# Layer 0's preparation: statistics from whole rows, weights by chunks, a compact bias table, scales spread from rows

## The chip, the core and the metric

The kernel runs on one core of one Trainium2 chip. The metric is the device time of one execution in microseconds. A core has five engines with queues of their own: PE (matrix products, with its weight loads shown as PEld), DVE (vector), ACT (scalar), POOL (general) and SP (which here only issues DMA transfers). ACT and POOL issue transfers too. An engine works through its queue in order, and waits at the head of the queue hold up everything behind.

## The reference

The input x is float32 of shape (4, 8, 512, 512). Four layers follow, each of the form x = x + layer(group_norm(x)). Layer 0, the only one that the change touches, is a spiking attention over T = 4 time steps, B = 8 images, N = 512 rows and D = 512 columns with H = 8 heads of 64. Its core is:

```python
def lif(x):            # over the time steps, state v
    v = v + (xt - v) / 2
    spike = v >= 1
    v = v * (1 - spike)

q = heads(lif(bn(x @ Wq.T, ...)))       # k and v likewise
scores = einsum('tbhnd,tbhmd->tbhnm', q, k) * D ** -0.5
scores = scores + bias_table[rel]       # rel = m - n + N - 1, per head
out = einsum('tbhnm,tbhmd->tbhnd', scores, v)
out = lif(out) * gate_scale + gate_shift
out = lif(bn(out @ Wp.T, ...))
```

Group normalisation takes the mean and the variance of two images (a group of G = 4 groups) at one time step. `bn` is batch normalisation with given statistics: g * (x - m) / sqrt(v + eps) + b. Layers 1 to 3 are convolutions of 13 x 13, 3 x 3 (quantised) and 3 x 3.

## The kernel before

`network` calls `layer0`, then the class `Layer1`, then `layers23`. Layer 0 works through 32 steps of one image b and one time step t, with t inside b. A step has four parts: the projections v, k and q (each 4 row or column chunks of 4 float32 products, in `project_in`), the attention (`attend`), and the output projection with the residual (`project_out`). In program order the attention of step n is followed by the projections of step n + 1, with the output projections of step n between them. A framework orders the instructions: it simulates the engines and on each engine issues, at any moment, the earliest instruction of the program that is ready, an instruction whose buffer isn't free being passed over. The order that comes out is fixed in the program. `tc.issue_after(op)` adds one rule: instructions of the block that run on the engine of `op` stand behind `op` there.

What the first steps need, and where it is in the code:

- **Batch norms** (`batch_norms`, L314 on): the 18 columns of parameters give `a_half` (half the scale, 4 projections x 4 chunks of 128 features) and `c_half` (half the offset), with the features on the partitions.
- **Scales along the free dimension** (`along_free`, L329 on): v, k and p need scale and offset along the columns, the same on all partitions. For each of the 4 chunks DVE multiplies the identity by a column of `a_half` or `c_half` (`diag`, L336, two buffers), and PE multiplies a matrix of ones by it (L337) into one PSUM bank, `ps_free`. `prepare_in` (L346 on) multiplies the weights of v or k by the scale (DVE, L349) and stores twice the offset as `c_twice` (ACT, L350). The weights of q are used as they are: its scale is on the partitions.
- **Weights** (`load_weights`, L304 on): the transposed matrix goes to `wT[n]`, 128 partitions x 4 chunks x 512. Partition q * 32 + a of chunk c holds row q * 128 + c * 32 + a. Each of four transfers fills one quarter q of the partitions, for all chunks.
- **The image of a step** (`load_quarters`, L417 on): it is loaded in four quarters, in pieces of 512 bytes, into a layout in which DVE transposes blocks of 32 x 32 (`transposed`, L477 on). One buffer, "xq". `transpose` first normalises it (L618).
- **Statistics** (`statistics`, L605 on): `bn_stats` on each of four pieces of both images of the group (`count`, L431), then two small PE products over the partitions, and a power on POOL (`group_stats`, L177 to L197). Image 0's pieces are taken from its quarters, the other image's from whole row chunks `xs` of 128 rows x 512, which share the 6 buffers of tag "x" with the residual's chunks `xr`.
- **Bias planes** (`prepare_bias`, L354 on): the bias of head h is a Toeplitz matrix. For `toep` it is split into three bf16 parts whose sum is the float32 value, for each of 8 heads as 128 partitions x 896 elements, in which partition p holds the table shifted by p. The kernel before loads each head's shifted rows in float32 (`hankel`), and then splits: ACT rounds (L365), DVE subtracts (L366), ACT rounds the rest (L367), POOL subtracts (L368), ACT rounds again (L369). `hankel` and `rest` have room for two heads each. They are in the space of tags "h_o" and "h_p", which become states of neurons afterwards.
- **Output weights** (`prepare_out`, L376 on): 32 small PE products give the `shift` that gate_shift brings (L382), DVE makes the offset `c` of it (L390 to L392), which is spread and stored as `c_twice["p"]` (L394). Then the scale is spread to `scale_p` (L398), and four chunks `wp_k` are scaled (DVE, L401) and split into two parts (ACT L405, DVE L406, ACT L407). `scale_p` and `wp_k` share the three buffers of tag "v" with the potentials of all neurons (`v_v`, `v_k`, `v_q`, `v_o`). The loaded `wp32` is in the buffer that later holds the attention's spikes `so`.
- **Bands for layer 1** (`bands1`, L709 on): their scratch takes the "h_p" space after the bias planes, and one PE product (L741) waits for loads into it.

The two matrix products of `attend` for a pair of heads j go into `ps_a` (one bank, L527) and `ps_b` (two banks, 24 products, L535); ACT copies `ps_a` into `v_o` at t = 0 (L545), and DVE adds `ps_b` (L550).

The order around the change is this one, in `layer0`:

```python
load(0)
load_weights("v", nc.sync)
statistics(0, 0, 0, as_rows(xs[0]))
statistics(0, 0, 1, load_x(1, 0, "xs"))
batch_norms()
for k in range(NC):
    transpose(0, k)
with tc.issue_after(prepare_in("v")):
    load_weights("k", nc.scalar)
    load_weights("q", nc.scalar)
```

After it come the projections of step 0. Their first product is followed by `prepare_in("k")` and the loads and statistics of the second time step; after the last follow `prepare_bias`, `prepare_out` and `bands1`, all held behind `prepare_in("k")`, the first product group and the first potential on their engines.

Of the kernel before, what the change touches and what calls it, by code (L numbers as in the profile page):

```python
# [34 lines left out]
F32 = mybir.dt.float32  # L35
# [8 lines left out]
P = 128  # L44
# [3 lines left out]
SQ = 32  # L48
# [218 lines left out]
def layer0(  # L267
# [36 lines left out]
    def load_weights(n, engine):  # L304
        rows = i[f"wT_{n}"].rearrange("(q c a) e -> q a c e", c=NC, a=SQ)
        for q in range(P // SQ):
            engine.dma_start(wT[n][q * SQ : (q + 1) * SQ], rows[q])
# [3 lines left out]
    ones = wpool.tile([P, P], F32, name="ones")  # L311
    nc.vector.memset(ones, 1.0)

    def batch_norms():  # L314

        neg_half = wpool.tile([P, 4, NC], F32, name="nh0")
        nc.vector.memset(neg_half, -0.5)
        nc.vector.tensor_scalar_add(a_half, bn[:, :, 3, :], EPS)
        nc.gpsimd.tensor_tensor(a_half, a_half, neg_half, op=ALU.pow)
        nc.vector.tensor_mul(a_half, a_half, bn[:, :, 0, :])  # L320
        nc.vector.tensor_scalar_mul(a_half, a_half, 0.5)
        c = c_half[:, :3, :]
        nc.vector.scalar_tensor_tensor(
            c, bn[:, :3, 2, :], -1.0, a_half[:, :3, :], op0=ALU.mult, op1=ALU.mult
        )
        nc.vector.scalar_tensor_tensor(
            c, bn[:, :3, 1, :], 0.5, c, op0=ALU.mult, op1=ALU.add
        )

    def along_free(cols):  # L330


        ps = ps_mm.tile([P, D], F32, tag="mm", name="ps_free")
        for c in range(NC):
            diag = work.tile([P, P], F32, tag="diag", name="diag", bufs=2)
            nc.vector.tensor_scalar_mul(diag, ident, cols[:, c : c + 1])  # L336
            nc.tensor.matmul(  # L337
                ps[:, c * P : (c + 1) * P], lhsT=ones, rhs=diag, start=True, stop=True
            )
        return ps  # L340

    def phases(x):
        return x.rearrange("p (v g) -> p g v", g=PH)

    def prepare_in(n):
        j = "qkvp".index(n)  # L346
        scale = along_free(a_half[:, j, :])
        for k in range(NC):
            nc.vector.tensor_mul(wT[n][:, k, :], wT[n][:, k, :], scale)  # L349
        return nc.scalar.mul(c_twice[n], along_free(c_half[:, j, :]), 2.0).ins  # L350

    def prepare_bias():


        n_u = toep[0].shape[2]
        table = i["table"]
        hankel = state.tile([P, 2, n_u], F32, tag="h_o", name="hankel")
        rest = state.tile([P, 2, n_u], F32, tag="h_p", name="rest")
        for h in range(H):
            src, r = hankel[:, h % 2, :], rest[:, h % 2, :]  # L360
            nc.scalar.dma_start(
                src, bass.AP(table.tensor, h * (2 * N - 1), [[1, P], [1, n_u]])
            )
            dst = [w[:, h, :] for w in toep]
            nc.scalar.copy(dst[0], src[:, ::-1])  # L365
            nc.vector.tensor_sub(r, src[:, ::-1], dst[0])  # L366
            nc.scalar.copy(dst[1], r)  # L367
            nc.gpsimd.tensor_sub(r, r, dst[1])  # L368
            nc.scalar.copy(dst[2], r)  # L369
# [6 lines left out]
    def prepare_out(wp32):  # L376
# [3 lines left out]
        for e in range(NC):  # L380
# [11 lines left out]
        nc.vector.scalar_tensor_tensor(c, bn[:, 3, 1, :], 0.5, c, op0=ALU.mult, op1=ALU.add)  # L392

        nc.scalar.mul(  # L394
            c_twice["p"].rearrange("p (g v) -> p g v", g=PH), phases(along_free(c)), 2.0
        )
        scale = work.tile([P, D], F32, tag="v", name="scale_p", bufs=3)
        nc.scalar.copy(scale, along_free(a_half[:, 3, :]))  # L398
# [243 lines left out]

    load(0)
    load_weights("v", nc.sync)
    statistics(0, 0, 0, as_rows(xs[0]))
    statistics(0, 0, 1, load_x(1, 0, "xs"))
    batch_norms()
# [7 lines left out]
    for n in range(-1, last + 1):  # L655
# [39 lines left out]
        if n < 0:  # L695
            with ExitStack() as behind:
                for op in first:
                    behind.enter_context(tc.issue_after(op))
                prepare_bias()
# [598 lines left out]
```

## Time and profile before

Three executions took 2936.95, 2939.79 and 2939.95 us. One more was profiled; the profile's times are from its first to its last instruction.

| what | us |
|---|---|
| median of three executions | 2939.79 |
| the profiled execution, its own time | 2938.79 |
| span of its profile | 2937.0 |
| PE busy in the span | 2833.3 (96%) |
| DVE busy | 2214.3 (75%) |
| POOL busy | 1035.3 (35%) |
| ACT busy | 551.2 (19%) |
| last output projection of layer 0 starts | 2049.3 |

Busy times are shares of the whole span. Stages differ in what limits them, so a stage is read by itself: how much of it each engine is busy, what the granted PE clock is, and what ended an engine's idle time. In the lists of instructions, a line names the engine, the line of the kernel, the operation, what it writes and reads, the count, and in brackets the idle time just before and what ended it. A letter q after an engine's name is its queue, where transfers are issued.

### The profile page before, as it was taken

Reading aid. Unit: us, or ns where it says so; the run is one execution under the profiler, and the core shown is the slowest. Engines: PE = TensorE matmul, PEld = TensorE weight load, DVE = VectorE, ACT = ScalarE, POOL = GpSimd, SP = SyncE. Lnnn points to the kernel's source line nnn. Section 1 sums busy time; section 2 is a strip of 40 time slices with the busy share of each in tenths; the row PEclk is TensorE's granted clock in tenths of the full one; section 3 lists DMA queues with packets and bytes.
Section 4 is the critical chain, followed back from the end, with each engine's and each line's share of the span. In section 5 each row is a group of like instructions: output and inputs, shape, how many; then the busy total and the mean of one; then the engine's idle time right before and its main releaser. Section 6 shows DMA issues by size and latency. Waiting matters only on the chain. (4 is left out here: it accounts for less than half of the span.)

```text
span 2937.0 us, 36614 instructions
## 1 busy us (share of the span) xinstructions
PE 2833.3 (96%) x12865; PEld 1303.7 (44%) x12865; DVE 2214.3 (75%) x3915; ACT 551.2 (19%) x859; POOL 1035.3 (35%) x1928
## 2 busy tenths in 40 slices
PE   6899999999999999999999999999999999589999
PEld 3454555554555545455455555455333333223334
DVE  7897788789779778878877886886655566887870
ACT  1300010011010001001001000110211112766664
POOL 3343234333234323323422433332211112676650
PEclk9899999999999999999999999999999999889999
DMA  7323322222222222222221122113877779698865
GB/s 180 97 81 81 76 58 66 66 73 77 69 61 70 71 75 73 58 66 66 76 68 46 49 54 55 51 42 95 226 194 216 201 208 247 142 204 209 222 171 147
DMA packets 323943, 322.10 MB, mean 110 GB/s; under 512 B 21639, under 2 KB 237391, under 8 KB 323647
## 3 DMA queue, kind: packets, MB, share of 16 engines
q1 hardware_dynamic: 261504, 236.70, 32.9%
q0 software_dynamic: 20192, 56.83, 6.2%
q10 hardware_dynamic: 42063, 26.23, 3.2%
q8 instruction: 101, 1.65, 0.2%
q14 instruction: 83, 0.68, 0.1%
HBM read 210.57 MB, written 103.60 MB: 107 GB/s over the span
## 5 line engine op out<-in xcount | busy, mean ns | idle before, releaser
L499 PE MATMUL ps_in<-w_v,xn 128*128 128x512 f32 x1024 | 459.7, 599 | 3.0 <-DVE xn L480 3.0
L499 PE MATMUL ps_in<-w_kq,xn 128*128 128x512 f32 x1024 | 450.2, 592 | 0.0
L815 PE MATMUL ps_conv<-x,bt 112*64 112x512 f32 x2048 | 445.1, 592 | 0.8 <-DVE v_p L467 0.8
L499 PE MATMUL ps_in<-xn,w_kq 128*128 128x512 f32 x1024 | 444.6, 592 | 0.0
L535 PE MATMUL ps_b<-toep,vtok 128*64 128x512 bf16 x3072 | 368.4, 383 | 1.0 <-DVE v_o L550 1.0
L475 POOL TENSOR_TENSOR h_v<-h_v,c_v 128x512 f32<-128x512 f32 x96 | 121.9, 1270 | 685.1 <-DVE h_v L474 659.4
L450 ACT ACTIVATE h_q<-v_q,c_half 128x512 f32<-128x512 f32 x96 | 69.2, 721 | 1473.0 <-DVE v_q L446 865.1
L584 POOL COPY x1s<-x1s 128x2 f32<-128x2 f32 (+1 forms) x1024 | 227.8, 278 | 272.8 <-DVE x1s L573 272.8
L562 PE MATMUL ps_out<-wp,so 128*128 128x512 f32 x1024 | 308.8, 444 | 0.0
L499 PEld LDWEIGHTS ps_in<-xn,w_kq 128*128 128x128 f32 x1024 | 194.3, 190 | 233.0 <-issue 222.0
L499 PEld LDWEIGHTS ps_in<-w_kq,xn 128*128 128x128 f32 x1024 | 194.2, 190 | 219.9 <-issue 205.0
L499 PEld LDWEIGHTS ps_in<-w_v,xn 128*128 128x128 f32 x1024 | 191.0, 191 | 218.6 <-issue 210.3
L815 PEld LDWEIGHTS ps_conv<-x,bt 112*64 112x64 f32 x2048 | 145.5, 135 | 289.7 <-issue 287.8
L1200 PE MATMUL ps_conv<-x,band_t 64*64 64x512 f32 x2040 | 252.5, 612 | 3.1 <-DVE band_t L1169 3.1
L1065 POOL COPY u<-x 128x512 f32<-128x512 f32 (+1 forms) x172 | 209.3, 1252 | 99.6 <-issue 51.8
L535 PEld LDWEIGHTS <-vtok 128*64 128x64 bf16 x3072 | 175.6, 111 | 154.7 <-issue 5.6
L562 PEld LDWEIGHTS ps_out<-wp,so 128*128 128x128 f32 x1024 | 192.6, 188 | 94.3 <-issue 58.3
L573 DVE SCALAR_TENSOR_TENSOR x1s<-v_p,xr 128x256 f32<-128x256 f32 x256 | 188.6, 776 | 13.9 <-DMA x<-x1s 3.1
L833 POOL DMA_DIRECT2D x<-xo x128 | 71.4, 565 | 313.7 <-ACT xo L822 299.4
L475 POOL TENSOR_TENSOR h_k<-h_k,c_k 128x512 f32<-128x512 f32 x96 | 123.2, 1283 | 135.1 <-DVE h_k L474 135.1
L822 ACT ACTIVATE xo<-ps_conv,off 128x512 f32<-128x512 f32 x128 | 87.9, 687 | 430.9 <-PE ps_conv L815 315.1
L1105 DVE SCALAR_TENSOR_TENSOR x<-ps_conv,inv,u 128x512 f32<-128x512 f32 (+1 forms) x172 | 121.7, 745 | 57.8 <-PE ps_conv L1098 30.6
(190 smaller groups left out, 3279.7 us busy)
## 6 DMA issues: line engine op xcount, KB each, us to landing
x<-x SPq DMA_DIRECT2D x64, 917.0 KB
x<-x SPq DMA_DIRECT2D x168, 256.0 KB
x<-x1s POOLq DMA_DIRECT2D x128, 262.0 KB, 2.6
xq<-in_x SPq DMA_DIRECT2D x128, 256.0 KB
xr<-in_x SPq DMA_DIRECT2D x128, 256.0 KB
out<-o SPq DMA_DIRECT2D x164, 192.0 KB
xs<-in_x SPq DMA_DIRECT2D x112, 256.0 KB
x<-xo ACTq DMA_DIRECT2D x128, 128.0 KB
```

The source lines that it names most:

```text
L475: nc.gpsimd.tensor_add(h, h, c_twice[n])
L499: mm = nc.tensor.matmul(ps, lhsT=lhsT, rhs=rhs, start=k == 0, stop=k == NC - 1)
L535: nc.tensor.matmul(pb[two * DH : (two + 1) * DH, :], lhsT=v[:, c, h * DH : (h + 1) * DH], rhs=toep[z][:, h, u : u + N], start=c == 0 and z ...
L562: nc.tensor.matmul(ps, lhsT=so[:, k, c * P : (c + 1) * P], rhs=wpT[z][:, k, :], start=k == 0 and z == 0, stop=k == NC - 1 and z == 1,)
L573: nc.vector.scalar_tensor_tensor(own, v.rearrange("p (g v) -> p g v", g=PH)[:, two, :], 1.0, by_phase[:, two, :], op0=ALU.is_ge, op1=ALU.add,)
L584: nc.gpsimd.tensor_copy(x1[:, f, u : u + n], x1[:, fm, um - n + 1 : um + 1][:, ::-1])
L815: mm = nc.tensor.matmul(ps[q * M1 : (q + 1) * M1, :], lhsT=bt[:, z, :], rhs=xt[:, w0 : w0 + N_PS1, z : z + NV], start=z == 0, stop=z == SH ...
L822: nc.scalar.activation(xo[:, a, :], ps, AF.Identity, bias=off[:, t : t + 1])
L833: engine.dma_start(bass.AP(dst.tensor, dst.offset + (q * n_half * W1_OUT * B + b) * D + f * NV, [[B * D, W1_OUT], [W1_OUT * B * D, n_half] ...
L1065: nc.gpsimd.tensor_copy(u[:n_p, j, :].rearrange("p (v g) -> p v g", g=PH), x[:, j, :].rearrange("p (g v) -> p v g", g=PH),)
L1105: done["DVE"] = nc.vector.scalar_tensor_tensor(own, ps[:n_p, :], w["inv"][:n_p], u[:n_p, j, :], op0=ALU.mult, op1=ALU.add, accum_out=sums[ ...
L1200: mm = nc.tensor.matmul(ps[j][b * HALF : (b + 1) * HALF, :], lhsT=band[half, b, dx, :], rhs=x3[half, s0 + j, dx : dx + D], start=dx == 0, ...
```

## The change

It touches five things, all in `layer0`:

- The statistics of the first time step are taken from whole row chunks of both images, so image 0 is loaded a second time as eight row chunks with the other image. These loads come before the quarters and the v weights in program order. `batch_norms` and the two transposes to rows come first of all, and the vector instructions of the block stand behind the last one of `batch_norms`.
- `load_weights` fills one chunk of all 128 partitions in each of its four transfers, for v, k and q.
- `along_free` takes rows: `as_rows_of` transposes the columns once on PE and copies them to SBUF on ACT, and PE then multiplies one column of the identity, repeated 128 times, by these rows.
- The bias table is split into its three parts in compact form, 24 partitions x 341 elements, on DVE (`split_bias`), and the parts are stored in DRAM. `prepare_bias` loads shifted rows of each part in bf16 for two heads at a time, and ACT copies them, reversed, to `toep`.
- In `prepare_out` the scale is spread before the offset.

```diff
     def load_weights(n, engine):
-        rows = i[f"wT_{n}"].rearrange("(q c a) e -> q a c e", c=NC, a=SQ)
-        for q in range(P // SQ):
-            engine.dma_start(wT[n][q * SQ : (q + 1) * SQ], rows[q])
+        rows = i[f"wT_{n}"].rearrange("(q c a) e -> c q a e", c=NC, a=SQ)
+        for c in range(NC):
+            engine.dma_start(wT[n][:, c, :], rows[c])
...
+    def as_rows_of(cols):
+        n = cols.shape[1]
+        ps = ps_mm.tile([n, P], F32, tag="mm", name="ps_rows")
+        nc.tensor.transpose(ps, cols, ident)
+        rows = wpool.tile([4 * NC, P], F32, tag="rows", name="rows", bufs=2)
+        nc.scalar.copy(rows[:n], ps)
+        return rows[:n]
+
+    def along_free(rows, j):
+        n = rows.shape[0]
         ps = ps_mm.tile([P, D], F32, tag="mm", name="ps_free")
         for c in range(NC):
-            diag = work.tile([P, P], F32, tag="diag", name="diag", bufs=2)
-            nc.vector.tensor_scalar_mul(diag, ident, cols[:, c : c + 1])
+            at = NC * j + c
             nc.tensor.matmul(
-                ps[:, c * P : (c + 1) * P], lhsT=ones, rhs=diag, start=True, stop=True
+                ps[:, c * P : (c + 1) * P], lhsT=ident[:n, at : at + 1].to_broadcast([n, P]),
+                rhs=rows, start=True, stop=True,
             )
...
-    def prepare_bias():
-        for h in range(H):
-            src, r = hankel[:, h % 2, :], rest[:, h % 2, :]
-            nc.scalar.dma_start(
-                src, bass.AP(table.tensor, h * (2 * N - 1), [[1, P], [1, n_u]])
-            )
-            dst = [w[:, h, :] for w in toep]
-            nc.scalar.copy(dst[0], src[:, ::-1])
-            nc.vector.tensor_sub(r, src[:, ::-1], dst[0])
-            nc.scalar.copy(dst[1], r)
-            nc.gpsimd.tensor_sub(r, r, dst[1])
-            nc.scalar.copy(dst[2], r)
+    def split_bias():
+        n_e = n_h // 3
+        parts = tc.dram_tile([3, H * n_h], BF16, name="bias_parts")
+        src = state.tile([3 * H, n_e], F32, tag="h_o", name="bias_table")
+        nc.scalar.dma_start(src, bass.AP(i["table"].tensor, 0, [[n_e, 3 * H], [1, n_e]]))
+        part = state.tile([3 * H, 3, n_e], BF16, tag="h_p", name="bias_part")
+        for z in range(3):
+            nc.vector.tensor_copy(part[:, z, :], src)
+            if z < 2:
+                nc.vector.tensor_sub(src, src, part[:, z, :])
+        nc.scalar.dma_start(
+            bass.AP(parts.tensor, parts.offset, [[n_e, 3 * H], [H * n_h, 3], [1, n_e]]), part
+        )
+        return parts
+
+    def prepare_bias(parts):
+        for h in range(0, H, 2):
+            for z in range(3):
+                hankel = state.tile(
+                    [P, 2, n_u], BF16, tag="h_o" if (h + z) % 2 else "h_p", name="hankel"
+                )
+                nc.scalar.dma_start(
+                    hankel,
+                    bass.AP(
+                        parts.tensor, parts.offset + (z * H + h) * n_h, [[1, P], [n_h, 2], [1, n_u]]
+                    ),
+                )
+                nc.scalar.copy(toep[z][:, h : h + 2, :], hankel[:, :, ::-1])
...
+        scale = work.tile([P, D], F32, tag="v", name="scale_p", bufs=3)
+        nc.scalar.copy(scale, along_free(a_rows, 3))
         nc.scalar.mul(
-            c_twice["p"].rearrange("p (g v) -> p g v", g=PH), phases(along_free(c)), 2.0
-        )
-        scale = work.tile([P, D], F32, tag="v", name="scale_p", bufs=3)
-        nc.scalar.copy(scale, along_free(a_half[:, 3, :]))
+            c_twice["p"].rearrange("p (g v) -> p g v", g=PH), phases(along_free(as_rows_of(c), 0)), 2.0
+        )
...
-    load(0)
-    load_weights("v", nc.sync)
-    statistics(0, 0, 0, as_rows(xs[0]))
-    statistics(0, 0, 1, load_x(1, 0, "xs"))
-    batch_norms()
+    normed = batch_norms()
+    a_rows = as_rows_of(a_half.rearrange("p n c -> p (n c)"))
+    c_rows = as_rows_of(c_half[:, :3, :].rearrange("p n c -> p (n c)"))
+    with tc.issue_after(normed):
+        for pair in range(PAIR):
+            statistics(0, 0, pair, load_x(pair, 0, "xs"))
+        load(0)
+        load_weights("v", nc.sync)
+        bias_parts = split_bias()
```

## The prediction

> **What bounds the kernel now.** I read the page's busy shares first: PE is busy 96% of the span, and the chain that ended last names PE lines, but only of the last 250 us, and the change ends before 140 us. So I cut the start into stages: to the first projection, the v projections of step 0, its k and q projections, its attention, and one steady step. Columns: stretch, its length, busy us of each engine (instructions), granted PE clock, share and rate of DMA.
>
> ```profile
> core 0: us, PE busy (x) PEld busy (x) DVE busy (x) ACT busy (x) POOL busy (x), PEclk, DMA share, GB/s
> 0.00:30.10 30.10, 5.93 (x21) 4.73 (x21) 14.71 (x43) 1.88 (x2) 4.96 (x9) 1.00 1.01 232
> 30.10:49.20 19.10, 17.85 (x48) 8.77 (x49) 13.79 (x28) 0.60 (x1) 3.65 (x3) 1.00 0.63 146
> 49.20:78.70 29.50, 28.55 (x70) 12.69 (x69) 29.14 (x43) 12.77 (x15) 16.47 (x11) 1.00 0.45 149
> 78.70:127.00 48.30, 34.31 (x192) 18.28 (x190) 38.48 (x74) 21.48 (x31) 8.10 (x5) 0.72 0.45 112
> 127.00:190.50 63.50, 63.39 (x257) 32.01 (x256) 56.30 (x96) 6.04 (x9) 25.98 (x49) 1.00 0.25 68
> ```
>
> From 127 us PE has no idle time (63.39 of 63.50), so whatever is saved before 127 us moves the end by as much. There are two holes: 30 us bound by DMA (share 1.01), and the 48.3 us attention, where PE is idle 14 us and slow at clock 0.72. In the first, the last loads of the other image come late, then follows a chain to the first projection (timeline, start and length in us):
>
> ```profile
> 16.41 0.69 DVE L431 BATCH_NORM_STATS2 st<-xs 128x6 f32<-128x512 f32 x1
> 21.56 1.36 DVE L431 BATCH_NORM_STATS2 st<-xs 128x6 f32<-128x512 f32 x2 [4.46 <-DMA xs<-in_x]
> 23.42 0.69 DVE L431 BATCH_NORM_STATS2 st<-xs 128x6 f32<-128x512 f32 x1
> 27.94 1.35 DVE L618 TENSOR_SCALAR xq<-xq,gmean_x,grstd_x 128x2048 f32<-128x2048 f32 x1 [0.66 <-POOL grstd_x L197]
> 30.09 5.78 PE L499 MATMUL ps_in<-w_v,xn 128*128 128x512 f32 x8 [3.00 <-DVE xn L480]
> ```
>
> SP's waits to 30 us say why they come late: their issue waited behind the k weights (total, times, longest).
>
> ```profile
> SPq L413 <- DMA w_kq<-in_wT_k: 6.7, 3, 5.4
> ```
>
> In the second hole the bias parts go round three engines, head by head, to 101 us (ns min/median/max, first and last start):
>
> ```profile
> L366 DVE TENSOR_TENSOR rest<-hankel,toep x8: 1075/1080/1743, 51.1 to 95.7; 128x896 f32<-128x896 f32 x8
> L368 POOL TENSOR_TENSOR rest<-rest,toep x8: 1880/1887/2292, 53.2 to 97.8; 128x896 f32<-128x896 f32 x8
> L369 ACT CAST toep<-rest x8: 921/938/942, 55.4 to 100.6; 128x896 bf16<-128x896 f32 x8
> ```
>
> and the output weights start only after scale_p, which stands behind c_p and so behind the shift matmuls at 78.7 us. They share the three "v" buffers with v_o:
>
> ```profile
> 95.45 0.60 ACT L394 ACTIVATE c_p<-ps_free 128x512 f32<-128x512 f32 x1 [1.23 <-PE ps_free L337]
> 100.08 0.59 ACT L398 COPY scale_p<-ps_free 128x512 f32<-128x512 f32 x1 [2.37 <-PE ps_free L337]
> 110.04 0.59 ACT L545 ACTIVATE v_o<-ps_a 128x512 f32<-128x512 f32 x1
> ```
>
> So the first v_o, which frees the one ps_a bank, waits till 110.
>
> [...] an out<-o store has 12 rows outermost, and 23 of them in 2901.1:2930 left 266 small completion packets beside 2169 of 2 KB (96 each), so about 12 each, where an xr load has 16:
>
> ```profile
> DMA packets 2437, 4.48 MB, mean 155 GB/s; under 512 B 266, under 2 KB 266, under 8 KB 2435
> q1 hardware_dynamic: 2435, 4.44, 53.3%
> out<-o SPq DMA_DIRECT2D x23, 192.0 KB
> ```
>
> [...] at 10 to 19 us the quarter loads of weights move 219 GB/s, at 20 to 24 us mostly whole-row xs loads 356 GB/s. [...] k<-v_k (L504) takes 0.41 us alone and 2.10 us at 69.96 beside POOL's L368.
>
> **The change part by part.**
>
> *Start.* Statistics now read 8 row chunks ahead of the quarters, so 4 MB instead of 3 MB come before the first projection. The "x" pool has 6 buffers: I expect SP to issue 6 chunks, then the 4 quarters and 4 weight chunks, which wait for no buffer, then the last 2 chunks, which wait for bn_stats. bn_stats now stand behind batch_norms on DVE (its last operation ends at 7.9 us); they began at 12.85, so that costs nothing. A weight chunk's source is 4 blocks of 32 rows that don't merge: [...] On those, in turn (a 2 KB packet takes 84 ns on an engine, a 512 B one 27): first data 2.1 us; 6 chunks x 8 packets x 84 ns = 4.0; constants about 1.0 (0.18 MB); quarters 4 x 32 x 27 ns = 3.5; w_v 4 x 32 x 84 ns = 10.8; last two chunks 1.3, receipt 0.5: 23.2 us. Then bn_stats 0.7, and from its end to the first projection 5.4 (6.0 before, less one w_v multiply of 0.6): 29.3 against 30.1, **-0.8**. The weights' DVE multiplies hide in this wait. If the load ran on 16 engines, w_v would take 2.7 and the start come 8 earlier; if the k and q chunks, on the same 4 engines, took turns with w_v, it would come about 9 later. I take packets in order of issue, since before the xs issued at 16.2 moved after the q weights issued at 14.6. k and q need 8 x 2.7 = 21.5 us more there, to about 45 to 48; q is needed at 63, k's last chunk by 37 to 38 at about its time of need. The second image's quarters queue behind (39 before, about 50 now); their bn_stats ran at 48.0, and four PSUM banks of 3.4 us each cover a stall of 2 to 3.
>
> *Table.* Its 33 KB load, five DVE operations on 24 partitions x 341 (about 0.35 us each by the 128x512 spike cast's 0.42), and the store fall in DVE's idle time before 23 us: nothing.
>
> *Scales.* 24 diag multiplies (0.28 us) leave DVE; matmuls stay as many; two transposes and two small ACT copies come in where nothing waits. PE waited 0.60 + 0.64 us for diags at 36.9 and 38.0: **-1.2** in the v stage.
>
> *k, q stage.* PE is dense already: 0. DVE loses 8 x 1.08 us of L366 and POOL 8 x 1.89 of L368 from here on, so DVE, saturated at 29.14 of 29.50, stops lagging: it read the last q bank at 85.45 though PE was done at 78.7.
>
> *Bias planes.* 12 loads of 448 KB (1792 B pieces) replace 8; 12 ACT copies of 1792 elements replace 24 of 896. Copy: 0.62 us at 512 and 0.94 at 896 give 0.83 ns per element, so 1.69 us; 20.3 in all against 22.5. The tags go h_p, h_o, h_p per pair of heads: h_p carries 8 tiles in series. A round is load (3.5 us from issue to the last completion record, 3.24 to 3.95 for five of the eight before) + 1.69 + 0.2 = 5.4; 8 rounds from 44 to 47 us end at 87 to 90, two per pair. Attention meets its fourth pair at about 92, so they are hidden.
>
> *Output weights.* scale_p no longer waits for the shift: its chain (4 x (1.13 + 0.67) DVE, 8 x 0.62 ACT) can run under the projections after wp lands at 54. v_o then waits for ps_a alone. The cost, a "v" buffer held during the projections, is covered while two buffers serve a 3.4 us PE group. Only the shift, c, one more transpose and copy remain late, and c_p is needed at the first output projection.
>
> *Attention.* PE work at full clock: shift 3.8, ps_b 4 x 2.78 = 11.1, kv 1.0, ps_a 8 x 0.2 = 1.6, spreads 16 x 0.19 = 3.0, bands 0.9, statistics 0.8, eight projection records 8 x 0.43 = 3.4: 25.6 of 48.3, so 22.7 can go. I leave 5: kvb (PE waits up to 2.3 for it in later steps) and part of the 6.7 us wait for the bands' load, which now follows the last h_p tile. **-17.7**.
>
> Sum -19.7. The profiled execution took 2938.79 us (span 2937.0 and 1.8 around), 1.0 under the median of 2939.79: **2919 us**.
>
> **Rivals.** *A, early start:* weights on all engines, or last chunks ahead of them: -8 more, 2911. For: before, loads blocked by buffers did delay others; against: the 12-engine store. *B, late start:* weights on 4 engines interleave with k and q: +9 and 1 of stalls, 2929. For: 12 chunks x 2.7 us on four engines; against: order of issue before. *C, slower:* the h_p series. With loads at 7.6 us, as the one issued at 85.62 took among others, a round is 9.5 and the last plane comes at 120; bands, and up to three pairs of ps_b behind them in PE's order, take some 18 more: 138 instead of 127, +11 less 2 from the start, 2948. It decides from 8.1 us a round (109 us). Against: five of the eight loads took 3.2 to 4.0 us, and only the first two, beside the 1 MB of wp, and this one more than 5.
>
> **How the numbers follow.** Forecast 0.50 (2913 to 2925), A 0.17, B 0.20, C 0.13. Within 0.2% is 2934 to 2946, about what a measurement of this kernel can tell from no change. Faster: 0.50 + 0.17 + 0.15 of B = 0.82; same 0.05 + 0.04 = 0.09; slower 0.09 of C. The range 2907 to 2935 leaves out C and the low end of A.
>
> **What would show it.** First projection at 29 us, with w_v multiplies spread to about 22 and four completions per weight load; planes done by 90; scale_p before 78; clock near 1.00 from 79 on; a steady step beginning near 107. Wrong if the first projection starts after 36, or PE waits for planes after 100.

## The result, and the profile after

The changed kernel is slower: 2946.57 us (median of 12 runs, 2942.63 to 2952.16) beside 2935.62 us for the kernel before (12 runs, 2930.96 to 2939.95). The ratio is 1.0035, with a 95% interval of 1.0027 to 1.0042: about 11 us more, where 20 us less were forecast. The profiled execution of the changed kernel took 2942.63 us, its span in the profile is 2940.8.

The first convolution of layer 1 starts at 2059.8 us instead of 2050.6, so 9.2 us of the loss lie in layer 0. The two profiled executions are only 3.8 us apart, because what follows (the execution's own time less that start) took 888.2 us before and 882.8 after. Nothing there is changed, and both lengths turn up in the kernels below (887.0 in e1_quarters, 883.1 in e5_bias_only), so I take this for spread between executions.

The stages, cut at the first projection, at the ends of v and of q, and at the first output projection, in the changed kernel. Columns: stretch, its length, busy us of each engine (instructions), granted PE clock, share and rate of DMA.

```profile
core 0: us, PE busy (x) PEld busy (x) DVE busy (x) ACT busy (x) POOL busy (x), PEclk, DMA share, GB/s
0.00:32.70 32.70, 5.65 (x22) 4.66 (x22) 11.98 (x34) 2.39 (x4) 4.95 (x9) 1.00 0.58 157
32.70:67.30 34.60, 24.06 (x49) 10.97 (x50) 15.30 (x26) 3.87 (x3) 3.80 (x3) 1.00 0.73 216
67.30:95.30 28.00, 28.00 (x71) 12.44 (x70) 24.59 (x46) 13.04 (x9) 7.24 (x6) 1.00 0.69 209
95.30:137.10 41.80, 37.27 (x203) 21.62 (x203) 27.67 (x62) 16.81 (x24) 1.06 (x2) 0.76 0.38 97
137.10:198.70 61.60, 61.49 (x253) 31.07 (x251) 55.21 (x93) 5.41 (x8) 25.44 (x49) 1.00 0.27 74
```

The kernel before, cut at the same places:

```profile
30.10:49.80 19.70, 18.45 (x49) 9.12 (x50) 14.39 (x29) 0.90 (x2) 3.91 (x3) 1.00 0.64 153
49.80:78.90 29.10, 28.15 (x71) 12.50 (x69) 28.74 (x42) 12.67 (x15) 16.21 (x10) 1.00 0.44 144
78.90:131.20 52.30, 38.31 (x201) 20.16 (x202) 41.78 (x82) 21.91 (x32) 9.28 (x7) 0.74 0.42 104
```

The start went from 30.1 to 32.7 us, but the v stage from 19.7 us to 34.6. In it PE is busy for 24 us only. The k and q stage has no gaps. The attention, from the end of the projections to the first output projection, takes 41.8 us instead of 52.3. So the change gains 10.5 us in one place and loses 17.5 in another (v ends at 67.3 instead of 49.8).

The 1.00 in the column of the clock is not a measurement everywhere. The trace's first record of the clock begins at 58.3 us in the changed kernel and at 34.3 in the one before, and a stretch without a record counts as 1.00. Up to just that point consecutive projection products start every 0.85 us, afterwards every 0.43. So PE ran at half rate to 58.3 us. The last chunk of w_v is scaled at 49.4; half of the time from there to 58.3 is 4.4 us, and half of 30.1 to 34.3 is 2.1. By this estimate some 2 us of the 17.5 are a later rise of the rate, and the rest is waiting.

What PE and SP waited for says where the loss is (waits of PE from 15 to 140 us, and of SP to 32 us: total, times, longest):

```profile
PE ps_in L523 <- DVE xn L504: 15.3, 1, 15.3
PE ps_in L523 <- DVE w_v L358: 10.5, 3, 4.0
...
PE ps_band L770 <- DMA bands<-in_w: 3.5, 1, 3.5
```

```profile
SPq L307 <- DMA w_kq<-in_wT_k: 13.2, 3, 8.8
```

The first wait names `xn`, but the transposes stand in DVE's order behind the first multiply of w_v, as the timeline shows (start and length in us; in brackets the idle time before and who ended it):

```profile
18.26 1.34 DVE L642 TENSOR_SCALAR xq<-xq,gmean_x,grstd_x 128x2048 f32<-128x2048 f32 x1 [0.66 <-POOL grstd_x L197]
31.37 0.69 DVE L358 TENSOR_TENSOR w_v<-w_v,ps_free 128x512 f32<-128x512 f32 x1 [11.76 <-DMA w_v<-in_wT_v]
31.98 2.48 DVE L504 STREAM_TRANSPOSE xn<-xq 128x512 f32<-128x512 f32 x4
37.06 0.69 DVE L358 TENSOR_TENSOR w_v<-w_v,ps_free 128x512 f32<-128x512 f32 x1 [2.60 <-DMA w_v<-in_wT_v]
42.60 0.69 DVE L358 TENSOR_TENSOR w_v<-w_v,ps_free 128x512 f32<-128x512 f32 x1 [4.86 <-DMA w_v<-in_wT_v]
48.72 0.69 DVE L358 TENSOR_TENSOR w_v<-w_v,ps_free 128x512 f32<-128x512 f32 x1 [5.43 <-DMA w_v<-in_wT_v]
```

The normalised image is ready at 19.6 us, 9.7 earlier than before (27.94 + 1.35): the statistics do come sooner. Then everything waits for weights, 5.5 to 6.1 us a chunk, and PE works in pieces:

```profile
32.74 2.08 PE L523 MATMUL ps_in<-w_v,xn 128*128 128x512 f32 x2 [15.33 <-DVE xn L504]
37.80 2.08 PE L523 MATMUL ps_in<-w_v,xn 128*128 128x512 f32 x2 [2.99 <-DVE w_v L358]
43.34 2.08 PE L523 MATMUL ps_in<-w_v,xn 128*128 128x512 f32 x2 [3.47 <-DVE w_v L358]
49.47 2.07 PE L523 MATMUL ps_in<-w_v,xn 128*128 128x512 f32 x2 [4.05 <-DVE w_v L358]
```

The view of the DMA from 20 to 50 us, in 40 slices, gives the reason. A digit is the busy share of the 16 engines in tenths; 2 is four engines of sixteen (0.25):

```profile
DMA  2222222222222222224932222267222226896222
GB/s 95 102 98 98 98 96 101 96 98 98 98 98 98 98 98 98 98 98 142 284 93 93 101 96 98 98 167 270 90 98 96 98 98 137 281 292 123 90 101 98
```

98 GB/s is the whole rate of the transfers of weights, about a quarter of what the packed weights of e2 reach below; only where an `xs` load is under way does it rise. By the completion records w_v's chunks landed at 31.4, 37.0, 42.6 and 48.7, and q's in between, at 32.9, 38.6, 44.1 and 50.1; k's had landed from 18.6 to 27.6. Each left four completions of engines where the loads by quarters left sixteen.

The attention, in ACT's timeline:

```profile
90.54 0.72 ACT L474 ACTIVATE h_q<-v_q,c_half 128x512 f32<-128x512 f32 x1 [6.79 <-DVE v_q L470]
91.17 1.67 ACT L393 COPY toep<-hankel 128x1792 bf16<-128x1792 bf16 x1
...
100.28 0.58 ACT L418 COPY scale_p<-ps_free 128x512 f32<-128x512 f32 x1 [0.72 <-PE ps_free L345]
...
110.79 1.69 ACT L393 COPY toep<-hankel 128x1792 bf16<-128x1792 bf16 x1 [0.77 <-DMA hankel<-bias_parts]
...
112.50 0.95 ACTq L755 DMA_DIRECT2D bands<-in_c  x1
...
116.34 0.59 ACT L569 ACTIVATE v_o<-ps_a 128x512 f32<-128x512 f32 x1
```

A copy of a plane stands behind `h_q`, which waits 6.8 us for q's neuron. scale_p comes at 100.3, after the projections and not under them. The last plane is done at 112.5, and in the same moment ACT issues the loads for the bands, which go into the same buffer and for which PE then waits 3.5 us.

### The profile page after: what moved, and what is told of

Its sections match the earlier page's. It is cut to its first block, busy times and chain, and to the rows that moved or that the text cites. A ratio compares the mean times of both kernels' runs of the same rounds, so it can differ in the third digit from the quotient of the medians.

```text
span 2940.8 us, 36579 instructions
## 1 busy us (share of the span) xinstructions
PE 2834.0 (96%) x12868; PEld 1305.1 (44%) x12868; DVE 2194.4 (75%) x3887; ACT 549.3 (19%) x850; POOL 1017.4 (35%) x1920
## 5 line engine op out<-in xcount | busy, mean ns | idle before, releaser
L1229 PE MATMUL ps_conv<-x,band_t 64*64 64x512 f32 x2040 | 246.4, 599 | 3.1 <-DVE band_t L1198 3.1
L586 PEld LDWEIGHTS ps_out<-wp,so 128*128 128x128 f32 x1024 | 192.6, 188 | 94.4 <-issue 57.6
L1127 PE MATMUL ps_conv<-xq,band 128*128 128x512 bf16 (+1 forms) x516 | 135.7, 401 | 27.2 <-DVE xq L1109 27.1
```

What stands on the lines that cost most here:

```text
L586: nc.tensor.matmul(ps, lhsT=so[:, k, c * P : (c + 1) * P], rhs=wpT[z][:, k, :], start=k == 0 and z == 0, stop=k == NC - 1 and z == 1,)
L1127: mm = nc.tensor.matmul(ps[:n_p, :], lhsT=w["band2"][:n_p, j, dx, :n_p], rhs=xq[:n_p, j, dx + 1 : dx + 1 + D], start=dx == 0, stop=dx == 2,)
L1229: mm = nc.tensor.matmul(ps[j][b * HALF : (b + 1) * HALF, :], lhsT=band[half, b, dx, :], rhs=x3[half, s0 + j, dx : dx + D], start=dx == 0, ...
```

## The experiments

All ratios are to the kernel before, run on the same chip beside them. Its median was 2936.52 us beside e1 to e4, 2932.63 beside e5 to e8, 2937.80 beside e9 to e11 and 2935.07 beside e12, so kernels of different groups are compared by their ratios. Times of landing are those of the trace's last completion record of a transfer. The theories on the start:

- **F**: a chunk load, whose source has 4 blocks outermost, runs on 4 engines (four completions, 98 GB/s); twelve such loads need 12 x 2.7 us there, 2.7 us being 256 KB at that rate.
- **O**: the order is at fault, w_v standing behind k and q; four engines would do.
- **S**: the second reading of image 0, or the statistics ahead of the quarters, delays the start.

**e1_quarters**: the changed kernel with the old loads of weights.

```diff
-        rows = i[f"wT_{n}"].rearrange("(q c a) e -> c q a e", c=NC, a=SQ)
-        for c in range(NC):
-            engine.dma_start(wT[n][:, c, :], rows[c])
+        rows = i[f"wT_{n}"].rearrange("(q c a) e -> q a c e", c=NC, a=SQ)
+        for q in range(P // SQ):
+            engine.dma_start(wT[n][q * SQ : (q + 1) * SQ], rows[q])
```

> The changed kernel with the old loads of weights (quarters of 32 partitions, 16 engines); all else as changed. Theory F (the chunk loads run on 4 engines and that makes v late): first v product at 26 to 30 us instead of 32.7 and the last of step 0 before 48 instead of 67.3, total 2928 to 2935 against about 2946.5. Theory S (the doubled reading of x and the statistics ahead are what costs): no gain, total 2944 to 2948.

Measured: 2923.97 us, ratio 0.9962 (0.9947 to 0.9977). First projection at 31.4 us, end of v at 50.0. The change without its chunk loads is faster than the kernel before, and by more than F had said (2928 to 2935), though the first projection is no earlier than before (F: 26 to 30).

**e4_chunks_only**: the kernel before with the chunk loads alone (the same edit the other way round).

> The kernel before with the chunk loads alone (4 engines), all else as before. F: v, k, q and the other image's chunks share four engines, first v product at 36 to 45 us instead of 30.1, total 2943 to 2952 against 2935.6. O: v comes ahead of k and q here, so the first product stays within 3 us of 30, total 2934 to 2940.

Measured: 2948.07 us, ratio 1.0044 (1.0027 to 1.0061): this one edit costs about what the whole change costs. The first projection starts at 37.4 us, v ends at 57.6, and then the k and q stage takes 39.1 us instead of 29.1. PE waits for statistics, whose images come late beside the weights (PE's waits, 15 to 110 us):

```profile
PE gps_x L180 <- DVE gsum_x L177: 29.6, 3, 19.7
```

The 19.7 us stand ahead of the first projection: the other image's four row chunks landed at 26.2 to 31.2, instead of 15.0 to 22.9. Another 8.8 us stand in the k and q stage, before the statistics of the next time step.

**e2_packed**: the changed kernel with v, k and q weights laid out in DRAM so that a chunk is 128 consecutive rows. The values and their number are the same; the input arrays are reordered to match.

```diff
-            engine.dma_start(wT[n][:, c, :], rows[c])
+            engine.dma_start(wT[n][:, c, :], i[f"wT_{n}"][c * P : (c + 1) * P, :])
```

> The changed kernel with the v, k and q matrices laid out in DRAM so that a chunk is 128 consecutive rows: the same four chunk transfers in the same order, each now on 16 engines with all 128 partitions. F: each load takes below 1 us of transfer, w_v is there by 25, step 0's v products end at 41 to 43, total 2921 to 2928. Theory O (not the engines but the place of w_v behind k and q in the queues costs): w_v still waits for k and q to be issued, v products end at 55 or later, total 2938 or more.

Measured: 2916.48 us, ratio 0.9938 (0.9923 to 0.9953). Sixteen completions a load; the chunks, w_v's and q's in turn, land 0.67 us apart. The windows and DVE's timeline of e2:

```profile
0.00:24.50 24.50, 5.65 (x22) 4.66 (x22) 12.02 (x34) 2.39 (x4) 4.96 (x9) 1.00 0.99 268
24.50:43.70 19.20, 18.92 (x49) 8.88 (x50) 14.87 (x26) 3.97 (x3) 3.81 (x3) 1.00 1.04 310
```

```profile
23.14 0.69 DVE L357 TENSOR_TENSOR w_v<-w_v,ps_free 128x512 f32<-128x512 f32 x1 [3.19 <-DMA w_v<-in_wT_v]
23.75 2.48 DVE L503 STREAM_TRANSPOSE xn<-xq 128x512 f32<-128x512 f32 x4
26.15 1.84 DVE L357 TENSOR_TENSOR w_v<-w_v,ps_free 128x512 f32<-128x512 f32 x3
```

The DMA share is 0.99 where it was 0.58, the rate 268 GB/s where it was 157, and the three later multiplies run in a row instead of one per 5.5 to 6.1 us. The transfers are as many and as large as in the change; only where the rows lie differs.

**e3_v_on_act**: the changed kernel with w_v loaded from ACT's queue, ahead of k and q.

```diff
-        load_weights("v", nc.sync)
+        load_weights("v", nc.scalar)
```

> The changed kernel with the v weights issued from ACT's queue, where they come before k and q; still chunks on 4 engines. O: w_v is there by 18 us, the first v product at 20 to 21, v ends by 40, total 2921 to 2928. F: w_v is early too but k's 4 chunks arrive at 27 to 30 and q's at 41, x chunks stick behind them on those engines, so that v ends at 42 to 46 and total is 2928 to 2935.

Measured: 2950.32 us, ratio 1.0054 (1.0039 to 1.0069), no better than the change itself. w_v landed from 10.8 to 21.8 us, about as early as O wants it (18). But the image came late. SP issued its quarters at 13.9 to 26.5 us instead of 3.7 to 12.2 in e2, three of SP's issues in that time, of two quarters and a row chunk, following within 0.1 us of the landing of a w_v chunk (13.91, 17.85, 21.84), and a quarter then took 8.9 to 12.2 us, not 6.2 to 8.1. I take this for a share on the same four engines, from an `xs` load of the changed kernel: twelve of its completions came at 35.6 to 36.1 us and four at 49.7 to 50.1, with those of q's last chunk. The last quarter landed at 36.8 us instead of 18.4, and the first projection started at 39.0. O's forecast falls: an earlier place for w_v here only moves the queue to the image. F's own numbers for this run (v ended by 42 to 46, 2928 to 2935 us) were as wrong: v ended at 58.2.

**e12_one_queue**: the changed kernel with all twelve chunks on SP, in the order v, k, q.

```diff
-    with tc.issue_after(prepare_in("v")):
-        load_weights("k", nc.scalar)
-        load_weights("q", nc.scalar)
+    prepare_in("v")
+    load_weights("k", nc.sync)
+    load_weights("q", nc.sync)
```

> The changed kernel with all twelve weight chunks on SP in the order v, k, q: still four completions a chunk, four engines each. Theory T (what cost the start is that two queues took turns on the same four engines, so that v's chunks came 5.6 us apart instead of 2.7): w_v chunks land 2.7 us apart, the last by 30 us, dense projections from 31 at the latest, v end at 48 to 52, ratio 0.995 to 0.999. Rival (four engines are too few in whatever order, since k and q need 21.5 us more): the k or q projections stall, q end later than 88 us, ratio above 1.000.

Measured: 2942.63 us, ratio 1.0027 (1.0019 to 1.0034), and F and O have half of it each. w_v landed at 20.0, 22.7, 25.4 and 28.0, 2.7 us apart: alone on its engines it needs half the time that it needed while q took turns with it. PE's timeline:

```profile
21.86 2.07 PE L523 MATMUL ps_in<-w_v,xn 128*128 128x512 f32 x2 [3.47 <-DVE xn L504]
24.21 3.03 PE L523 MATMUL ps_in<-w_v,xn 128*128 128x512 f32 x4 [0.28 <-DVE w_v L358]
28.80 1.13 PE L523 MATMUL ps_in<-w_v,xn 128*128 128x512 f32 x2 [1.56 <-DVE w_v L358]
...
42.23 7.89 PE L523 MATMUL ps_in<-w_kq,xn 128*128 128x512 f32 x18
71.73 0.58 PE L180 MATMUL gps_x<-gsum_x,avg 128*128 128x1 f32 x2 [21.61 <-DVE gsum_x L177]
```

The first projection starts 8 us earlier than in the kernel before, and v ends at 42.4 instead of 49.8. Then PE stands for 21.6 us, in front of a product for the next step's statistics. Its images are queued behind q's chunks, the last of which landed at 58.6 us, and they landed themselves at 59.6 to 73.0. The q projections end at 94.9, later than 88 as the rival had it. So both are shown: taking turns doubles the time of w_v (5.5 to 6.1 us a chunk instead of 2.7), and in either order tried, w_v beside q or w_v first, twelve loads on four engines made somebody late (v by 17.5 us at its end, the next image by 21.6 us of PE).

**e11_sixteen_loads**: the changed kernel with each chunk loaded by four transfers of 32 rows, so that 32 rows stand outermost. The arrays are as in the change.

```diff
         for c in range(NC):
-            engine.dma_start(wT[n][:, c, :], rows[c])
+            for q in range(P // SQ):
+                engine.dma_start(wT[n][q * SQ : (q + 1) * SQ, c, :], rows[c, q])
```

> The changed kernel with each chunk loaded by four transfers of 32 rows each, so that the outermost size is 32 and each runs on 16 engines; the arrays are as in the change. Theory F (the four engines of a chunk load are the whole loss): first projection at 25 to 31 us, no waits of 5 us between the v records, v end at 44 to 50, ratio 0.993 to 0.997. Rival (sixteen transfers of 64 KB in place of four of 256 KB choke on their issue, or the eight completion semaphores in turn couple SP to the k and q loads): first projection later than 36 and ratio above 0.999.

Measured: 2927.25 us, ratio 0.9962 (0.9949 to 0.9975). Sixteen completions per transfer, as for the quarter loads of before, which have 32 rows outermost too; first projection at 25.3 us, v's end at 49.7. The same bytes from the same rows to the same places, in four times as many transfers, and the loss is gone. Its v stage takes 24.4 us, though, against 19.2 in e2. The sixteen issues of w_v last from 18.2 to 27.0, and the DMA moved 211 GB/s from 18 to 30 us, where e2's moved 386 from 18 to 26. PE's half rate lasted to 41.1 us, against 30.0 in e2: half of the 10.3 us by which it lasted longer after the first projection is 5.2, which by this estimate is the whole difference.

**e10_packed_alone**: the kernel before with the packed chunks of e2 and nothing else of the change.

> The kernel before with the packed weight chunks alone: 128 consecutive rows each, 16 engines. If the gain of the packed kernel at the start (24.5 us instead of 30.1 to the first projection) is due to 16 engines on the weights, this one starts at 25 too, the rest as before, time 5 to 6 us below before, ratio 0.998. If it needs the statistics ahead of the quarters as well, it starts at 28 to 30 and the ratio is 0.999 to 1.000.

Measured: 2927.97 us, ratio 0.9970 (0.9958 to 0.9982). First projection at 25.7 us, against 24.5 in e2. So S falls, and the change's own idea for the start isn't shown to give anything: with the statistics ahead the image is ready sooner, but the first projection comes 1.2 us earlier beside packed weights and 1.3 later beside quarters (e1: 31.4 against 30.1). Both are within the spread of single profiles: in e2, e7, e8 and e9, which differ only in what comes later, it starts at 24.5, 26.6, 23.3 and 25.1.

The attention was then taken apart. Theory **P** puts its gain down to the bias planes, **W** to the output weights; **H** puts what remains of it down to the loads in the "h_p" buffer.

**e5_bias_only** and **e6_scales_only**: the kernel before with one part each. Of the edits only the calls are shown; the functions come with them as in the change.

```diff
+    bias_parts = split_bias()
...
-                prepare_bias()
+                prepare_bias(bias_parts)
```

> The kernel before with the compact bias split and the 12 hankel loads alone; weight loads, statistics and scales stay as they were. Theory P (the bias planes, which went round three engines, carry most of the shorter attention): start at 30 us, v stage and q end as before (50 and 79 within 1), attention 7 to 9 us shorter than before's 52.3 from the end of the projections to the first output projection, time 8 us below before, 2928. Theory W (the output weights' chain carries it): attention shorter by 3 at most, time within 3 us of before.

```diff
-        scale = along_free(a_half[:, j, :])
+        scale = along_free(a_rows, j)
...
+        nc.scalar.copy(scale, along_free(a_rows, 3))
         nc.scalar.mul(
```

> The kernel before with the scales spread from rows, and scale_p ahead of the shift, alone. Theory P: v stage 1.2 us shorter (no diag waits), attention within 2 us of before because the scale's four matmuls still stand on PE behind the last projection, time 1 to 3 us below before, 2934. Theory W, my forecast's reason for much of its 17.7: scale_p before 78 us, the weights' chain under the projections, attention 8 us shorter, 2927.

Measured: e5 2930.38 us, ratio 0.9992 (0.9984 to 1.0000); e6 2928.32 us, ratio 0.9982 (0.9975 to 0.9988). The attention is 45.3 us in e5 and 42.8 in e6. Alone, the planes give 7.0 us of it and the scales 9.5; together, in e1, they give 8.6. They don't add, and neither theory is right. (One profile stands for each kernel. In e4 and e10, which leave the attention as it was, it took 49.5 us and not 52.3, so about 3 us of such a difference can have other causes.) e6 gained what W expected without W's reason: scale_p came after the projections, which end at 80.3 us (ACT's timeline of e6):

```profile
89.84 0.56 ACT L402 COPY scale_p<-ps_free 128x512 f32<-128x512 f32 x1
```

Why they don't add can be read from the traces, in us after the end of the projections:

| kernel | scale_p | output weights done | first v_o | last plane | bands on PE | first output projection |
|---|---|---|---|---|---|---|
| before | 21.2 | 31.2 | 31.1 | 22.6 | 28.3 | 52.3 |
| e5, bias alone | 11.8 | 23.8 | 23.9 | 21.1 | 26.0 | 45.3 |
| e6, scales alone | 9.5 | 27.9 | 23.6 | 15.9 | 25.2 | 42.8 |
| e1, both | 6.6 | 22.8 | 22.9 | 18.9 | 23.6 | 43.7 |
| after | 5.0 | 21.1 | 21.0 | 17.2 | 21.2 | 41.8 |
| e2, packed | 6.1 | 21.6 | 21.5 | 17.6 | 21.6 | 41.3 |
| e7, in turn | 11.1 | 22.0 | 21.9 | 11.2 | 16.1 | 37.9 |
| e8, scale early | before the end (at 32.1 us) | 18.5 | 20.3 | 17.5 | 20.9 | 39.8 |
| e9, e7 and e8 | before the end (at 34.2 us) | 16.8 | 16.9 | 9.6 | 17.2 | 39.4 |

The first `v_o` comes within 0.1 us of the end of the output weights in all rows but two (e6, 4.3 earlier; e8, 1.8 later), and each part alone brings it from 31 to 24 us. What one part frees the other would have freed too; the bands and the copies of planes among those of the weights on ACT then stand in the way of both. That last reading is from the table, not from a run that takes both away. Of e5's and e6's gain a part was lost at the ends: their first projections were 1.8 and 1.5 us later than before's, and 2.6 and 2.7 us were lost again in the steps after the attention. In time e5's gain is therefore hardly clear of none.

**e7_alternate**: e2 with the hankel buffers in strict turn, six tiles each, the last one in "h_o".

```diff
-                    [P, 2, n_u], BF16, tag="h_o" if (h + z) % 2 else "h_p", name="hankel"
+                    [P, 2, n_u], BF16, tag="h_o" if (h // 2 + z) % 2 else "h_p", name="hankel"
```

> The packed kernel (2916.5 us) with the two hankel buffers taken strictly in turn, so that each carries 6 loads in series, not 8 and 4, and the last is in h_o and not in the buffer that the bands need. Theory H (the series of loads in h_p, and the bands' loads queued behind its last tile, hold the attention): PE's wait of 5.5 us for the bands goes, last plane some 8 us earlier (81 instead of 89), attention 4 to 6 us shorter than 41.3, time 2912. Rival (the copies stand in ScalarE's order behind the spikes of q, so the loads hardly matter): last plane within 3 us of 89 and time within 2 us of 2916.5.

**e8_scale_early**: e2 with the scale computed after k's, and c_p after the output weights.

```diff
                     first += [prepare_in("k"), did, potentials[0]]
+                    nc.scalar.copy(c_twice["p"], along_free(a_rows, 3))
...
-        scale = work.tile([P, D], F32, tag="v", name="scale_p", bufs=3)
-        nc.scalar.copy(scale, along_free(a_rows, 3))
+        scale = c_twice["p"]
```

> The packed kernel with scale_p computed right after the scales of k, at about 25 us, and held in the tile of c_p, which is written after the output weights are done. Theory W: the chain of the output weights starts before the end of the projections (72 us) and v_o is not late any more: attention 3 to 6 us shorter than 41.3, time 2912. Theory H: the chain comes at most 2 us earlier because VectorE's order and the planes hold it, the wait for the bands stays at 5 us, time within 2 us of 2916.5.

**e9_both**: both edits.

> The packed kernel with both: hankel buffers in strict turn (ratio 0.9928 to before alone) and scale_p early (0.9933 alone), the packed kernel itself 0.9938. If the two waits are separate, the attention takes 36 us from the end of the projections to the first output projection (41.3 packed, 37.9 and 39.8 with one of them), PE's wait for the bands stays under 1 us and the ratio is 0.992, 2910. If they are one wait seen twice, 38 us and the ratio of the first, 0.993.

Measured: e7 2913.50 us, ratio 0.9928 (0.9915 to 0.9942); e8 2914.84, ratio 0.9933 (0.9921 to 0.9946); e9 2917.68, ratio 0.9938 (0.9925 to 0.9950). PE's wait for the bands, in e2, e7 and e8 in turn:

```profile
PE ps_band L769 <- DMA bands<-in_w: 5.5, 1, 5.5
```

```profile
PE ps_band L769 <- DMA bands<-in_w: 0.9, 1, 0.9
```

```profile
PE ps_band L768 <- DMA bands<-in_w: 7.6, 1, 7.6
```

H is right on the place: with the buffers in turn the last plane comes 6.4 us earlier after the projections, and most of the wait goes (a later one, of `ps_sum` for the bands, grew from 0.5 to 2.7 us). The attention is 3.4 us shorter; in the time the medians differ by some 3 us (0.9938 to 0.9928), but the intervals overlap, so a gain isn't shown. e8 shows why an early scale helps little: it is there at 32 us and not at 25 as planned, long before the projections end at 70.5, but the first output weight still comes 5 us after them, since DVE has its multiplies in order behind q's neurons and behind `c_half`, which waits for the shift; and the wait for the bands grew by 2.1 us. e9 missed: the attention stayed at 39.4 us, PE waited 2.2 us for the bands where under 1 was expected, and the ratio is that of e2. e2, e7, e8 and e9 are not told apart by these runs; all four beat both kernels, by 0.6 to 0.7% over the one before.

## Why the prediction was wrong

**The step that failed** is in the start, in two sentences: "I expect SP to issue 6 chunks, then the 4 quarters and 4 weight chunks, which wait for no buffer", and "I take packets in order of issue".

- *The place in the queue.* SP issued 6 row chunks, 2 quarters, 2 row chunks, 2 quarters, and only then w_v, at 21.3 to 27.6 us. Its chunks wait for no buffer, but SP waited 13.2 us for landings of k's chunks, which ACT had issued from 12 us on: the issues at 21.31, 24.14 and 27.59 wait each for the semaphore on which a chunk of k had landed just before, at 21.29, 24.13 and 27.57. I had counted waits for buffers and not those for earlier transfers to complete, although the line `SPq L413 <- DMA w_kq<-in_wT_k: 6.7, 3, 5.4` shown in the prediction is one.
- *Turns.* I took the order from one case in the trace of before, where xs and q ran on sixteen engines (sixteen completions each). Here SP's and ACT's chunks landed in turn (31.4, 32.9, 37.0, 38.6 us): 5.5 to 6.1 us between w_v chunks with q's between them, 2.7 us in e12 with nothing between. Nor was it the order of issue: q's first chunk was issued at 15.7 us and w_v's first at 21.3, and w_v's landed first, at 31.4 against 32.9.
- *The size.* The start was put at -0.8 us. It measured +2.6 at the first projection and +17.5 at the end of v. This was rival B's mechanism, at 9 us and 0.20. B doubled the 10.8 us of w_v; in fact w_v came last of all, together with q. Twelve chunks x 2.7 us are 32.4, and from 16.6, where the last quarter has landed, that is 49.0: w_v's last chunk landed at 48.7, q's at 50.1. The prediction also had all of w_v in place before the first projection; PE began with the first chunk alone at 32.7, so the first projection looks less late than the weights were. I had this sum ("12 chunks x 2.7 us on four engines") and gave q the end of it, with "q is needed at 63", as if w_v were served first.

That a chunk load takes four engines was an estimate in the prediction, taken from a store with 12 rows outermost that left about 12 completions each in the trace of before. It was right (four completions, 98 GB/s), and e1, e2 and e4 show that the chunk loads alone turn the sign; e11, which only splits them, that it is the four engines. I had priced it and then hidden it behind an order that was an assumption. e12, which has w_v first and alone, shows that the order I assumed would not have saved it either: the next image queues behind (21.6 us of PE, where the prediction had a cover of "2 to 3"). In e3, where w_v goes first of all, the image is late instead: its last quarter landed at 36.8 us, against 18.4 in e2.

**Right or nearly**: the statistics ahead and the table cost nothing at the start that shows, and gave nothing (e1, e10). The copy of 1792 elements took 1.69 us, as worked out. The k and q stage stayed dense. The diag waits are gone from the v stage, but not seen in its sum, which the weights set.

**The attention** gave 10.5 us and not 17.7. Of its points:

- *Planes by 87 to 90*: last one at 112.5, 17.2 after the projections. A part is the later start; in e2, which starts on time, it is 89.3, at the forecast's own hour, but there the projections end 7 us earlier. Rounds were stretched where copies stood behind `h_q` on ACT, a queue that I had not looked at: one plane's rows had landed at 86.8 and were copied from 91.2. PE did not wait for planes, so rival C's price did not fall due; what came of the series in "h_p" was the wait for the bands, most of which e7 takes away.
- *scale_p before 78*, that is, under the projections: wrong in every kernel but e8 and e9. Its products stand on PE behind the last projection; e8 shows that they can run 38 us earlier, and that this step was worth little.
- *5 us left of 22.7, clock near 1.00*: this is the term that was mis-sized. In the windows of the attention PE was idle for 4.5 us (41.8 less 37.27), as forecast, but its clock was 0.76:

```profile
95.30:100.00 4.70, 4.70 (x39) 4.64 (x39) 4.26 (x11) 2.31 (x2) 0.00 (x0) 0.92 0.81 244
100.00:106.70 6.70, 6.70 (x35) 4.14 (x33) 3.48 (x6) 3.33 (x5) 0.00 (x0) 0.50 0.81 160
106.70:113.00 6.30, 6.30 (x43) 2.87 (x42) 2.77 (x5) 4.84 (x8) 0.00 (x0) 0.78 0.20 74
113.00:118.50 5.50, 1.95 (x10) 1.53 (x9) 4.67 (x10) 2.24 (x4) 0.00 (x0) 0.80 0.40 96
118.50:124.00 5.50, 4.52 (x19) 2.22 (x21) 3.81 (x13) 1.23 (x2) 0.00 (x0) 0.50 0.56 143
124.00:130.00 6.00, 6.00 (x45) 2.71 (x41) 2.29 (x5) 2.17 (x4) 0.00 (x0) 0.78 0.03 8
```

Busy time x (1 - clock), line by line, is 0.4 + 3.4 + 1.4 + 0.4 + 2.3 + 1.3 = 9.1 us. With the idle time that makes 13.6 us left, against the 5 that I left. That the low clock was a mere consequence of the waits that would go was my estimate, and no run showed it: the largest of these terms, 3.4, lies in a stretch in which PE had no wait at all.

From the end of the projections to the end of layer 0 the balance is: 16.4 us later at q's end, 10.5 back in the attention, 5.9 later at the first output projection. Another 3.3 us were lost in the steps after: 1.8 of them in one step, which took 65.9 us instead of 64.1 at clock 0.97, around a 2.2 us wait of PE for kvb. Those steps are unchanged. The clock records show what goes with it: in the changed kernel the clock fell to 0.50 for 3.4 us twice, from 246.1 and from 1239.3 us, each time just after such a wait, and in the kernel before never in these steps. Half of 6.8 us is 3.4. The other kernels agree but for one: from the first to the last output projection those with two such falls (after, e3, e5, e9) took 1921.1 to 1922.6 us and those with none or one 1916.0 to 1918.8, but e6, with one, 1921.2. Why a kernel has the falls I have no experiment on, and leave it open.

## What to carry to other kernels

A transfer is priced by the engines that it can use, and in these runs that number went with how the source is laid out (4 blocks outermost: four completions, 2.7 us; 128 rows outermost: sixteen, 0.67 us): ask it of each load, then add up all loads that are confined to the same few engines, whichever queue issues them, and take the sum as the time of each of them until the order is shown. A queue that "waits for no buffer" may still wait for the landing of another queue's transfers (SP did here for 13.2 us). When two parts of a change each remove a wait in the same stage, their gains need not be a sum (7.0 and 9.5 us alone, 8.6 together); and a stage in which PE was slow-clocked need not get its full clock back because waits are gone (0.74 before, 0.76 after).

## What the runs showed of the hardware

- The load of 256 KB on four engines (four completions) took 2.7 us when nothing else was on them (e12: 20.0, 22.7, 25.4, 28.0), 98 GB/s; the same bytes as 128 consecutive rows landed every 0.67 us (e2, sixteen completions), 390 GB/s. Four transfers of 32 rows each (e11) ran on sixteen engines again (sixteen completions each), though at 211 GB/s in all and not at e2's 386.
- A transfer with sixteen completions landed late beside chunks: in the changed kernel an `xs` load issued at 33.0 us had twelve completions at 35.6 to 36.1 and the last four at 49.7 to 50.1, with the four of the last q chunk (49.4 to 50.1).
- Projection products started every 0.85 us up to the first record of the clock and every 0.43 after it (records begin at 34.3 us in before, 58.3 in after, 41.1 in e11, 30.0 in e2), where the table of windows says 1.00 throughout.
- The granted PE clock fell to 0.50 at 99.3 us and stayed there past 106.7, in a stretch that the profile shows as busy from end to end. It fell after 32 products of one column each (95.1 to 98.8 us), during eight small spreads (98.7 to 100.2). No run varies them, so what made it fall is not shown.
